# A graph layer with gathered tiles: the first two units swapped, and the first residual loads issued at the end of the first stage

## The chip, the cores and the metric

One core of one Trainium2 chip. The metric is the time of one execution in microseconds (us) on the device; each number is a median with its range over several executions. Ratios are computed as the mean time of one kernel's fast runs over the mean of the other's fast runs of the same rounds, with a 95% interval, so they are not quite the ratio of the medians quoted.

## The reference, cut to what matters

```python
B, N, F_IN, F_OUT = (8, 4096, 256, 256)
HW = jnp.einsum('bnf,fo->bno', H, W)
A_norm = jax.nn.relu((A + A.T) * 0.5)
D = jnp.sum(A_norm, axis=1)
D_safe = jnp.where(D > 0, D, 1.0)
d_inv_sqrt = jnp.where(D > 0, D_safe ** (-0.5), 0.0)
DAD = d_inv_sqrt[:, None] * A_norm * d_inv_sqrt[None, :]
L_norm = jnp.eye(N, dtype=H.dtype) - DAD
out = jnp.einsum('nm,bmo->bno', L_norm, HW)
return jax.nn.relu(out)
...
x = _layernorm(x + _L0_gnn_ref(x, L0_gnn_W, adj), axis=-1)
```

The adjacency A is sparse. The 4096 nodes are 32 blocks of 128 rows.

## The kernel before: the parts that matter

In the first stage the adjacency is symmetrised on VectorE and written to HBM, superblock by superblock (four blocks each). The degrees follow from row sums. x times W is scaled by `r`, the inverse root of the degree, and written to HBM as `g_dram`. The last ten blocks are formed before their degree is known: they are *held*, and `release` scales and writes them once it is. Block 0's output is summed along the way in a PSUM tile, `lead`.

```python
for i in range(NS):
    for j in range(i, NS):
        ...                               # load, symmetrise, sum rows
    degrees(i)                            # deg, none, e, r, minus_r, minus_e
    for m in range(i * A, (i + 1) * A):
        if m in held:
            release(m)                    # scale by r, write to g_dram, queue its matmuls into lead
    ...
    elif i < 6:
        pieces = spread_early(i - 4)      # index lists of unit 0, then of unit 1
        for n in range(5):
            due.append([1 + n // 2, next, (pieces, None)])
        due.append([1 if i == 5 else 4, collect_index, (i - 4,)])
```

In the second stage the other 31 blocks are done in 16 *units* of two (the last of one). Each unit has some 20 tiles. A tile is two gathers started by GpSimd: 128 rows of the adjacency (`ga`) and 128 rows of `g_dram` (`g`, 1 MB) into one of 13 ring buffers. TensorE multiplies them into `py`. A block is then evicted by ScalarE, added to its residual rows `xr` (1 MB of x), normalised and written.

```python
def residual(i, ypool):
    xr = ypool.tile([P, B, F], F32, tag="xr", name=f"xr_{i}", bufs=4)
    nc.scalar.dma_start(xr, x[:, i * P : (i + 1) * P, :].rearrange("b p f -> p b f"))
    return xr
...
ring = [gath.tile([P, G], F32, tag=f"g{k}", name=f"g{k}", bufs=1) for k in range(RING)]   # RING = 13
steps = [(u, step) for u in range(NU) for step in steps_of(u)]
...
for n in range(RING):
    gather(n)
xr = {}
...
after(3, residuals, [0])                  # xr of block 0, issued by ScalarE
finish(0)                                 # evict lead
for q, (u, step) in enumerate(steps):
    if new:
        after(10 if u + 1 < NU else 4, residuals, range(2 * u + 1, 2 * u + 1 + blocks(u)))
```

## Time and profile before

| | before |
|---|---|
| median of 3 runs | 1635.83 us (1634.33 to 1635.96) |
| end of the first stage (last matmul of `lead`) | 586 us |
| sixth gathered tile landed | 613.8 us |
| TensorE without a gap | 613.9 to 1001 us |

The lines these come from are shown and read in the prediction below. A windows line reads: stretch, length, then busy time of each engine with its number of instructions, then granted TensorE clock (1.00 is full), DMA share and GB/s.

### The profile page before, as it was taken

The page shows a single profiled execution, that of the slowest core. Times are in us where ns is not written, and L with a number is a line of the kernel's source. Part 1 is how long each engine was busy: PE and PEld are TensorE (multiplying, and loading weights), DVE is VectorE, ACT ScalarE, POOL GpSimd, SP SyncE. Part 2 cuts the span into 40 slices and gives each one's busy share as a digit, 9 for nine tenths or more (in the row PEclk, how much of TensorE's full clock was granted, in tenths as well). Part 3 has the DMA queues.
Part 4 walks back from the last instruction along what each step waited for, and adds up shares of the span by engine and source line. Part 5 has one row for each costly group of instructions (what it writes and reads, how often), then busy time and mean ns, then how long its engine had stood idle before and what let it go on. Part 6 is the DMA issues. An engine that isn't in the chain of part 4 may idle for free.

```text
span 1631.2 us, 18596 instructions
## 1 busy us (share of the span) xinstructions
PE 1491.2 (91%) x6544; PEld 787.1 (48%) x6544; DVE 810.5 (50%) x1886; ACT 365.0 (22%) x454; POOL 792.8 (49%) x1116
## 2 busy tenths in 40 slices
PE   6999989898899969999999999897979989999893
PEld 5787877776677624334343333333323333343331
DVE  5666578665465530052616527525635624545244
ACT  3555545444444410010100100100001001010110
POOL 3010010101011156477777767767767767777662
PEclk9999999999989989999999999999999999999997
DMA  9999999998788699889999999999999899999995
GB/s 352 374 370 389 392 375 376 400 368 333 290 320 329 258 360 405 298 291 397 327 404 377 370 370 379 365 367 349 345 361 337 323 382 335 378 387 369 357 355 188
DMA packets 229715, 575.13 MB, mean 353 GB/s; under 512 B 20473, under 2 KB 119081, under 8 KB 191945
## 3 DMA queue, kind: packets, MB, share of 16 engines
q0 software_dynamic: 56672, 305.12, 48.9%
q1 hardware_dynamic: 100912, 134.23, 23.4%
q10 hardware_dynamic: 72032, 134.51, 22.0%
q8 instruction: 55, 0.90, 0.2%
q14 instruction: 44, 0.36, 0.1%
HBM read 479.07 MB, written 136.34 MB: 377 GB/s over the span
## 4 chain that ended last, share of the span: by engine, by line
PE 57%; DMA 23%; issue 7%; DVE 6%; POOL 5%; ACT 1%; POOLq 0%; SPq 0%; DVEq 0%; ACTq 0%
PE py L805 34%; DMA g<-g_dram,gi 18%; PE pg L437 10%; PE lead L400 5%; PE tr L342 3%; PE xtr L426 3%; DVE sym L345 2%; DMA a_dram<-sym 2%; POOL g L663 2%; POOL ga L652 2%; DMA xin<-in_x_dram 1%; DMA adj<-in_adj_dram 1%; DVE part L350 1%; ACT sym L349 1%; POOL rstd L589 1%
## 5 line engine op out<-in xcount | busy, mean ns | idle before, releaser
L805 PE MATMUL py<-g,ga 128*64 128x512 f32 (+1 forms) x3152 | 938.3, 607 | 71.7 <-DMA g<-g_dram,gi 60.6
L805 PEld LDWEIGHTS py<-g,ga 128*64 128x64 f32 (+1 forms) x3152 | 350.8, 156 | 646.5 <-issue 630.5
L663 POOL DMA_INDIRECT g<-g_dram,gi x302 | 341.9, 1132 | 199.6 <-DMA g<-g_dram,gi 67.4
L652 POOL DMA_INDIRECT ga<-a_dram,ai x302 | 327.9, 1086 | 96.1 <-issue 83.4
L565 ACT ACTIVATE y<-py,minus_r 128x512 f32<-128x512 f32 x120 | 78.5, 687 | 922.5 <-PE py L805 646.9
L591 DVE TENSOR_SCALAR xr<-xr,mv,rstd 128x256 f32<-128x256 f32 x256 | 89.4, 419 | 299.1 <-POOL rstd L589 299.1
L437 PE MATMUL pg<-w_sb,xt 128*128 128x256 f32 x1024 | 231.8, 385 | 0.9 <-DVE sym L345 0.9
L437 PEld LDWEIGHTS pg<-w_sb,xt 128*128 128x128 f32 x1024 | 196.0, 194 | 29.3 <-issue 2.4
L345 DVE TENSOR_TENSOR sym<-tr,adj 128x512 f32<-128x512 f32 x256 | 163.7, 684 | 81.3 <-PE tr L342 77.9
L350 DVE TENSOR_REDUCE part<-sym 128x32 f32<-128x2048 f32 x64 | 145.5, 2281 | 61.1 <-ACT sym L349 61.0
L395 POOL DMA_DIRECT2D strip<-a_dram x32 | 18.3, 573 | 316.4 <-PE lead L400 309.8
L342 PE MATMUL tr<-ident,adj 128*128 128x128 f32 x1024 | 135.9, 283 | 21.3 <-DMA adj<-in_adj_dram 10.7
L349 ACT ACTIVATE sym<-sym 128x2048 f32<-128x2048 f32 x64 | 122.5, 1915 | 117.6 <-DVE sym L345 111.8
L342 PEld LDWEIGHTS tr<-ident,adj 128*128 128x128 f32 x1024 | 118.4, 145 | 49.6 <-DVE sym L345 22.5
L576 DVE TENSOR_TENSOR xr<-xr,y 128x2048 f32<-128x2048 f32 (+1 forms) x35 | 73.7, 2106 | 69.5 <-ACT y L565 64.6
L167 DVE TENSOR_TENSOR_SCAN incl_r<-carry,lists 128x32 f32<-128x32 f32 x13 | 2.8, 219 | 196.0 <-PE lists L236 196.0
L426 PE MATMUL xtr<-ident,xin 128*128 128x128 f32 x512 | 74.6, 292 | 21.9 <-DVE sym L345 18.2
L581 DVE BATCH_NORM_STATS2 stats<-xr 128x6 f32<-128x256 f32 x256 | 87.2, 411 | 0.8
L370 POOL TENSOR_TENSOR r<-e,neg_half 128x4 f32<-128x4 f32 x8 | 8.3, 1041 | 161.7 <-DVE e L369 155.6
L267 DVE TENSOR_TENSOR hot<-iota_q,at 128x1024 bf16<-128x1024 f32 x64 | 76.4, 1219 | 14.1 <-PE lead L400 12.9
L400 PE MATMUL lead<-gt,strip 128*128 128x512 f32 x176 | 83.3, 593 | 0.0
L427 ACT COPY xt<-xtr 128x512 f32<-128x512 f32 x128 | 69.3, 589 | 49.9 <-PE xtr L426 48.8
(104 smaller groups left out, 639.8 us busy)
## 6 DMA issues: line engine op xcount, KB each, us to landing
adj<-in_adj_dram SPq DMA_DIRECT2D x64, 1024.0 KB, 10.6
a_dram<-sym ACTq DMA_DIRECT2D x64, 1024.0 KB, 9.4
xin<-in_x_dram SPq DMA_DIRECT2D x64, 512.0 KB, 11.6
xr<-in_x_dram ACTq DMA_DIRECT2D x32, 1024.0 KB, 25.0
out_dram<-xr SPq DMA_DIRECT2D x31, 1024.0 KB, 24.4
g_dram<-gt ACTq DMA_DIRECT2D x22, 1024.0 KB, 7.0
g_dram<-held ACTq DMA_DIRECT2D x10, 1024.0 KB, 9.7
ga<-a_dram,ai POOLq DMA_INDIRECT x302, 9.6
```

What stands on the lines that cost most here:

```text
L342: nc.tensor.transpose(pt[:, c * P : (c + 1) * P], tji[:, c, a * P : (a + 1) * P], ident)
L345: nc.vector.tensor_add(sym[:, a, :], pt, tij[:, a, :])
L349: nc.scalar.activation(sym, sym, AF.Relu, scale=0.5)
L350: nc.vector.tensor_reduce(part[:, i * A : (i + 1) * A, j * S // Q : (j + 1) * S // Q], sym.rearrange("p a (c q) -> p a c q", q=Q), AX.X, A ...
L400: nc.tensor.matmul(lead[c], lhsT=strip, rhs=g[:, c * S : (c + 1) * S], start=not done, stop=len(done) == NB - 1, skip_group_check=True,)
L426: nc.tensor.transpose(pt[:, k, c, :], xin[b // H][:, b % H + k, c * P : (c + 1) * P], ident)
L437: nc.tensor.matmul(pg[:, k * FO : (k + 1) * FO], lhsT=xt[:, b + k, c, :], rhs=w_sb[:, c, :], start=(c == 0), stop=(c == FC - 1),)
L581: nc.vector.bn_stats(stats[:, b, :], z[:, b, :])
L591: ins = nc.vector.tensor_scalar(z[:, b, :], z[:, b, :], mv[:, b, 0:1], rstd[:, b : b + 1], ALU.subtract, ALU.mult,)
L652: tail["pool"] = nc.gpsimd.indirect_dma_start(out=at if both else at[:, :P], out_offset=None, in_=a_pairs if both else a_rows, in_offset=b ...
L663: tail["pool"] = nc.gpsimd.indirect_dma_start(out=gt, out_offset=None, in_=g_dram, in_offset=bass.IndirectOffsetOnAxis(ap=gi[:, t : t + 1] ...
L805: tail["pe"] = nc.tensor.matmul(py[2 * u + 1 + b][c][rows, :], lhsT=at[:, off + rows.start : off + rows.stop], rhs=gt[:, c * S : (c + 1) * S],
```

## The change

It is meant to fill idle DMA time at the boundary of the stages and to keep the boundary's gathers free of other loads. The residual rows of block 0 and of the first unit are now loaded by SyncE's queue, before the first gathers. And the units go in the order 1, 0, 2, 3 and on, unit 1 having 24 tiles and unit 0 having 29. The diff, cut to its core (`prepare` and `lists` only get the new order's names):

```diff
+SEQ = [1, 0, *range(2, 16)]
...
-                for u in range(3):
-                    due.append([1 + u, count_place_rest, (u,)])
+                for n, u in enumerate(SEQ[:3]):
+                    due.append([1 + n, count_place_rest, (u,)])
             elif i < 6:
-                pieces = spread_early(i - 4)
+                pieces = spread_early(SEQ[i - 4])
...
-                due.append([1 if i == 5 else 4, collect_index, (i - 4,)])
+                due.append([1 if i == 5 else 4, collect_index, (SEQ[i - 4],)])
...
-    def residual(i, ypool):
+    def residual(i, ypool, engine=None):
...
-        steps = [(u, step) for u in range(NU) for step in steps_of(u)]
+        steps = [(u, step) for u in SEQ for step in steps_of(u)]
...
+        xr = {
+            i: residual(i, ypool, nc.sync) for i in (0, *range(2 * SEQ[0] + 1, 2 * SEQ[0] + 1 + blocks(SEQ[0])))
+        }
         for n in range(RING):
             gather(n)
-        xr = {}
...
-        after(3, residuals, [0])
         finish(0)
...
-                after(10 if u + 1 < NU else 4, residuals, range(2 * u + 1, 2 * u + 1 + blocks(u)))
+                if q > 0:
+                    after(10 if u != SEQ[-1] else 4, residuals, range(2 * u + 1, 2 * u + 1 + blocks(u)))
```

More of the change, by code (lines that the diff above doesn't have):

```diff
@@ L554 @@
                 pass
-    def residual(i, ypool):
+    def residual(i, ypool, engine=None):
         xr = ypool.tile([P, B, F], F32, tag="xr", name=f"xr_{i}", bufs=4)
-        nc.scalar.dma_start(xr, x[:, i * P : (i + 1) * P, :].rearrange("b p f -> p b f"))
+        (engine or nc.scalar).dma_start(xr, x[:, i * P : (i + 1) * P, :].rearrange("b p f -> p b f"))
         return xr
@@ L731, in residuals @@
                     xr[i] = residual(i, ypool)
+        ahead = {u: {k: SEQ[n + k] for k in (2, 3, 4) if n + k < NU} for n, u in enumerate(SEQ)}
         def prepare(u):
-            if u + 2 < NU:
+            if 2 in ahead[u]:
+                v = ahead[u][2]
                 for _ in spread(
-                    u + 2,
-                    lpool.tile([P, NB, P], BF16, tag="hot", name=f"hot_{u + 2}", bufs=1),
-                    lpool.tile([P, NB, tmax], F32, tag="inn", name=f"inn_{u + 2}", bufs=1),
-                    lpool.tile([P, NB, 2, tmax], BF16, tag="val", name=f"val_{u + 2}", bufs=1),
-                ):
-                    pass
-            if u + 4 < NU:
-                patterns(u + 4)
+                    v,
+                    lpool.tile([P, NB, P], BF16, tag="hot", name=f"hot_{v}", bufs=1),
+                    lpool.tile([P, NB, tmax], F32, tag="inn", name=f"inn_{v}", bufs=1),
+                    lpool.tile([P, NB, 2, tmax], BF16, tag="val", name=f"val_{v}", bufs=1),
+                ):
+                    pass
+            if 4 in ahead[u]:
+                patterns(ahead[u][4])
         def lists(u):
@@ L751, in lists @@
             pr = one[:, w : w + 2 * NB].rearrange("p (k m) -> p k m", k=2)
-            if u + 4 < NU:
-                count(u + 4, tot, low)
-            if u + 3 < NU:
-                count_rest(u + 3, pr[:, 0], pr[:, 1])
-            if u + 2 < NU:
-                pl = two[:, w : w + 2 * tiles[u + 2]].rearrange("p (k t) -> p k t", k=2)
-                collect(u + 2, pl)
-                index(u + 2, pl)
-            if u + 3 < NU:
-                place_rest(u + 3, pr[:, 0], pr[:, 1])
-            if u + 4 < NU:
-                place(u + 4, tot, low)
-        after(3, residuals, [0])
+            if 4 in ahead[u]:
+                count(ahead[u][4], tot, low)
+            if 3 in ahead[u]:
+                count_rest(ahead[u][3], pr[:, 0], pr[:, 1])
+            if 2 in ahead[u]:
+                v = ahead[u][2]
+                pl = two[:, w : w + 2 * tiles[v]].rearrange("p (k t) -> p k t", k=2)
+                collect(v, pl)
+                index(v, pl)
+            if 3 in ahead[u]:
+                place_rest(ahead[u][3], pr[:, 0], pr[:, 1])
+            if 4 in ahead[u]:
+                place(ahead[u][4], tot, low)
         finish(0)
```

## The prediction

> **What bounds the kernel now.** I read the page first, then a table by stage, then the chain of waits around the change of stage, then the waits of TensorE and GpSimd in the second stage. The page says that this is a kernel in which two things are nearly full at once:
>
> ```profile
> PE   6999989898899969999999999897979989999893
> PEclk9999999999989989999999999999999999999997
> DMA  9999999998788699889999999999999899999995
> ```
>
> The first stage (adjacency symmetrised, x multiplied by W, block 0 summed) ends at about 586 us; the second (302 gathered tiles of 1 MB, in 16 units) fills the rest. Both PE and DMA read 9 nearly everywhere in the second stage, so I split it, with PE busy, its clock, the DMA share and GB/s as the columns to watch:
>
> ```profile
> 555.00:558.00 3.00, 0.97 (x32) 0.85 (x31) 3.00 (x5) 1.97 (x1) 1.00 (x1) 1.00 0.32 125
> 558.00:570.00 12.00, 11.91 (x28) 5.44 (x29) 9.60 (x22) 4.45 (x4) 4.25 (x9) 1.00 1.02 405
> 570.00:582.00 12.00, 12.00 (x29) 5.33 (x28) 3.10 (x6) 3.50 (x2) 2.20 (x4) 1.00 1.01 403
> 582.00:585.00 3.00, 3.00 (x8) 1.33 (x7) 0.00 (x0) 1.37 (x2) 0.00 (x0) 1.00 0.80 320
> 585.00:588.00 3.00, 0.82 (x2) 0.00 (x0) 2.03 (x2) 1.37 (x2) 2.31 (x2) 1.00 0.20 28
> 588.00:600.00 12.00, 1.96 (x4) 0.34 (x4) 10.44 (x24) 0.00 (x0) 9.87 (x8) 0.62 1.03 372
> 600.00:614.00 14.00, 10.27 (x34) 3.25 (x36) 0.00 (x0) 0.00 (x0) 10.32 (x11) 0.84 1.03 403
> 614.00:665.00 51.00, 51.00 (x123) 21.82 (x124) 2.87 (x8) 0.00 (x0) 35.91 (x36) 0.97 1.00 389
> 665.00:705.00 40.00, 40.00 (x138) 14.64 (x137) 3.06 (x4) 2.75 (x4) 17.88 (x17) 1.00 0.73 267
> 705.00:782.00 77.00, 77.00 (x292) 30.03 (x291) 27.84 (x89) 4.81 (x7) 53.57 (x47) 1.00 0.95 364
> 782.00:1000.00 218.00, 218.00 (x922) 83.06 (x922) 110.99 (x334) 19.44 (x29) 166.45 (x145) 1.00 0.99 371
> 1000.00:1600.00 600.00, 546.09 (x2126) 209.45 (x2123) 271.63 (x826) 51.46 (x80) 425.22 (x372) 0.97 0.96 359
> ```
>
> Three regimes are to be seen. From 586 to 614 TensorE starves while DMA is full. From 614 to 1000 PE is busy in every microsecond, so PE sets the pace. From 1000 on PE has gaps (546 of 600 us) and DMA is at 0.96: DMA sets it. The chain of waits shows where the first regime ends, and the PE stretches of units 0 and 1 after it:
>
> ```profile
> 603.44 10.33 DMA g<-g_dram,gi
> 613.77 0.14 issue
> 613.90 90.87 PE py L805 x254
> ...
> 705.93 76.03 PE py L805 x256
> ```
>
> The gather issued at 603.44 is the sixth; the first five were issued from 586.73 on. Once it has landed, at 613.77, PE never waits again until 1001. So the landing of the sixth gather is the number that a change at the boundary must move. GpSimd's waits between 655 and 710 us tell what the DMA's dip there is:
>
> ```profile
> POOL g L663 <- PE py L805: 21.4, 8, 4.6
> ```
>
> GpSimd waits for PE to free one of the 13 ring buffers: the ring is full, and DMA is idle because PE is slower there, not for want of anything to fetch.
>
> [...] the three residual loads, issued on ScalarE's queue from 585.87 to 588.85 us, landed 6.4, 14.4 and 32.2 us after issue, beside gathers whose own latency was 8.3 to 11.3 us (median 10.0) until 615, against a median of 5.8 between 675 and 706 where DMA has room. [...] GpSimd's gather instructions take about 1.0 us elsewhere but 1.4 to 2.9 us while VectorE works between 586 and 595.
>
> **The change part by part.**
>
> *Residuals moved.* Three loads of 1 MB (blocks 0, 1, 2, from 585.87) leave the boundary. Three others (0, 3, 4; blocks 3 and 4 are the first unit's now) go to SyncE's queue, idle after its last input load at 524.37, and start when their buffers come free. These take over memory of the first stage, in its adjacency buffers. The last users there are the index matmuls that end at 556.7 and the last symmetrising adds on VectorE, which end at 563.2. So I expect one load at about 551 to 557 and the rest from 563.
>
> What do they meet there? Ten held tiles of 1 MB are written to HBM; eight of them are issued between 558.07 and 575 and the last lands at 585.46, on which the first gather waits (GpSimd waits 7.9 us for it, to 585.38). The table shows DMA share 1.02 and 1.01 from 558 to 582. So 3.1 MB at 405 GB/s, 7.8 us of all engines, goes into a stretch that is full, and not into the hole of 540 to 558, unless a buffer is freed early.
>
> *What that is worth.* Count DMA work up to the landing of the sixth gather. It is nearly the same set of bytes before and after; what can be won is idle time. From 557 on that is: one microsecond at share 0.32, 0.7 us; 582 to 585 at 0.80, 0.6 us; 585 to 588 at 0.20, 2.4 us. Sum 3.7 us. The hole at 585 to 588 is the restart between the last write and the first gather's packets; it does not vanish, because the first gather still waits for the writes, but it moves and may be partly filled by late residual packets; I give back 1.5 us for it. The third old load landed only at 619, after the sixth gather, so a part of it, some 0.25 MB or 0.6 us, was not in the old count and is in the new. Sum: 3.7 - 1.5 - 0.6 = 1.6 us earlier.
>
> *Check by the issue side.* With the loads in the way, the last held write lands some 5 to 6 us later, at 591, and the first gather's issue goes from 586.73 to about 592.5. The sixth comes five pairs later: 5 x 2.56 us (0.94 + 0.30 + 1.00 + 0.30, plus rounding, from the undisturbed pairs) = 12.8 us, plus about 1.5 us for VectorE's remaining interference: 606.8. With the unloaded latency of 5.8 us it lands at 612.6, or 1.2 us earlier. Both ways say 1 to 2 us.
>
> *Order 1, 0.* Both units begin with the same seven half tiles, so the starving start is alike. PE time of the two together is a sum, 90.87 + 76.03 and the same first steps, whatever the order. What the order moves is when the ring fills. Before, unit 0 (29 tiles, seven of the dearest kind) came first and filled the ring by 665; DMA then lost (1 - 0.73) x 40 = 11 us. After, unit 1 (24 tiles) needs about 24 x 2.8 = 67 us of DMA plus one 1 MB output in 76 us of PE; it stays fed but gains only some 6 tiles of lead; unit 0 then brings the ring to its cap of 13. Either way the ring is about full when both are done, so the lost 11 us are not recovered: the later starvation is put off only by lead carried over, and that is capped. I book 0, with 1 tile, 2.8 us, either way.
>
> *The rest.* Index lists keep their places by position in the order; the removed issue slots on ScalarE (0.4 us each) were not on the chain. 0.
>
> Sum: -1.6 us at the boundary. It should carry through to the end, since both regimes after it start earlier by the same amount with the same ring. From 1635.8 this gives 1634. Because the residual buffer freed first might catch the hole before 558 (1 MB there is worth 2.6 us), I lean a little lower: 1633.
>
> **The rivals.** First, full relief: the loads land without delaying the writes. Then gathers start at 586.73 with no residuals beside them; GpSimd issues the sixth at 603.44 as before, and it lands 5.8 us later, at 609.2: 4.6 us won, 1631. For it speaks the share of about 0.3 to 0.6 before 558; against it the buffers' release at 563. Second, the loads turn into a longer wait for the held writes: 7.8 us later gathers with a second clock ramp of PE (granted clock 0.62 between 588 and 600) gives a loss of 3 to 5 us, 1640. For it speaks the saturated stretch; against it the same 3.1 MB missing later. Third, the order keeps DMA busy where it idled and the whole 11 us come back at the end: 1623. Against it speaks the cap of 13 buffers.
>
> **Range and chances.** The terms are a few microseconds each, against a spread of 1.6 us in the three runs. I take 1633, with 1626 to 1639 for 8 times in 10. Two per cent is 33 us; no term above, nor all together in either direction, comes to that: faster 0.02, same 0.96, slower 0.02.
>
> **What would show it right or wrong.** Right: residuals issued by SyncE between 550 and 575; the last held write and with it the first gather some 5 us later than 586.7; the first gathers with a latency of 6 to 8 us in place of 10; PE unbroken from about 612 on; the full-ring dip at 665 to 705 gone or moved to about 740 to 780. Wrong: first gather at 586.7 (then the first rival); PE gaps inside unit 1 (the ring runs dry, slower); DMA share clearly higher from 614 to 800 and the first starvation much later than 1001 (the third rival).

## More of the kernel before

Different sessions fell on different chips; their numbers (3, 8, 9, 12, 15) are used as names only.

The source line numbers move between kernels, because lines were added; names are what to go by.

## The result, and the profile after

The changed kernel took 1652.62 us (median of 4 runs, 1651.29 to 1654.05); the kernel before 1635.89 (4 runs, 1634.33 to 1640.65, three of them from earlier, one from that session). The ratio is 1.0097, interval 1.0074 to 1.0121. This is within 2%, but 13.6 us above the top of the predicted range, and the sign is the other one.

The profile of that run, busy tenths in 40 slices of the span, to set beside the lines of the same names at the head of the prediction:

```profile
PE   6999989898899868999999999989988989999894
PEclk9999999999899987999999999999999999999997
```

The sixteenth slice (620 to 661 us) has PE at 8 with a granted clock of 7; before, both were 9. One window of the same kernel (columns as before) says how much:

```profile
614.00:665.00 51.00, 42.89 (x90) 16.46 (x87) 2.86 (x8) 0.00 (x0) 33.72 (x34) 0.83 0.99 385
```

Before, TensorE was busy for all 51 us with 123 matmul passes; here it did 90 passes, and unit 2 starts at 811.2 us instead of 797.0. The profiled executions have spans of 1652.3 and 1631.2 us, so 14.2 of 21.1 us are lost by then and 7 later. The timeline of PE in that window (start, length, what, and in brackets the idle time before it and what ended it) shows how:

```profile
621.11 14.21 PE L815 MATMUL py<-g,ga 128*128 128x512 f32 x32 [0.16 <-DMA g<-g_dram,gi]
636.83 0.59 PE L815 MATMUL py<-g,ga 128*128 128x512 f32 x1 [1.51 <-issue]
638.93 1.01 PE L815 MATMUL py<-g,ga 128*128 128x512 f32 x1 [1.51 <-issue]
...
651.58 36.26 PE L815 MATMUL py<-g,ga 128*128 128x512 f32 x111 [1.11 <-issue]
```

Passes that are normally 0.43 us apart start 0.8 to 2.8 us apart. Most of their distances are multiples of 0.70 us (636.83, 638.93: 3 x 0.70). "issue" means that the profile shows nothing that the engine waited for; a wait whose release was not recorded would read the same, and records are missing in this trace, as is told below. But all the passes of one tile need the same two gathers, and these gaps lie inside a tile, so it is no late tile. The clock of 0.83 comes from 17.1 us at half clock (granted 0.50) that begin at 638.7, four us after the slow stretch began. TensorE had been busy for 1.18 of the 4.0 us before (634.7 to 638.7), so I take the half clock for a consequence; that is my reading, and no run isolates it. A good part of the loss comes through it: the gaps themselves sum to 7.5 us. TensorE, not DMA, is what was late: DMA was at 0.99.

Nothing in the diff acts on a running matmul. So the first question was whether this belongs to the kernel at all, and the second what the change does where it does not happen.

### The profile page after: what moved, and what is told of

Same layout as the page of the kernel before. It is cut to its first block, busy times and chain, and to the rows that moved or that the text cites. A ratio compares the mean times of both kernels' runs of the same rounds, so it can differ in the third digit from the quotient of the medians.

```text
span 1652.3 us, 18595 instructions
## 1 busy us (share of the span) xinstructions
PE 1504.6 (91%) x6544; PEld 791.3 (48%) x6544; DVE 812.1 (49%) x1886; ACT 364.6 (22%) x454; POOL 783.8 (47%) x1116
## 4 chain that ended last, share of the span: by engine, by line
PE 58%; DMA 22%; issue 7%; DVE 6%; POOL 5%; ACT 2%; POOLq 0%; SPq 0%; DVEq 0%; another core or an unknown queue 0%; ACTq 0%
PE py L815 37%; DMA g<-g_dram,gi 15%; PE pg L439 9%; PE lead L402 5%; DMA a_dram<-sym 4%; PE tr L344 3%; PE xtr L428 3%; DVE sym L347 2%; POOL ga L654 2%; DMA xin<-in_x_dram 2%; POOL g L665 2%; DMA adj<-in_adj_dram 1%; DVE part L352 1%; ACT sym L351 1%; POOL rstd L591 1%
## 5 line engine op out<-in xcount | busy, mean ns | idle before, releaser
L815 PE MATMUL py<-g,ga 128*64 128x512 f32 (+1 forms) x3152 | 950.7, 607 | 74.9 <-DMA g<-g_dram,gi 48.0
L815 PEld LDWEIGHTS py<-g,ga 128*64 128x64 f32 (+1 forms) x3152 | 355.5, 155 | 657.4 <-issue 639.2
L665 POOL DMA_INDIRECT g<-g_dram,gi x302 | 336.8, 1115 | 214.1 <-PE py L815 78.1
L654 POOL DMA_INDIRECT ga<-a_dram,ai x302 | 323.1, 1070 | 96.5 <-issue 83.7
L344 PE MATMUL tr<-ident,adj 128*128 128x128 f32 x1024 | 136.3, 283 | 20.9 <-DMA adj<-in_adj_dram 10.2
L428 PEld LDWEIGHTS xtr<-ident,xin 128*128 128x128 f32 x512 | 60.7, 149 | 41.6 <-DVE sym L347 29.2
```

Source lines behind the costliest of these rows:

```text
L344: nc.tensor.transpose(pt[:, c * P : (c + 1) * P], tji[:, c, a * P : (a + 1) * P], ident)
L428: nc.tensor.transpose(pt[:, k, c, :], xin[b // H][:, b % H + k, c * P : (c + 1) * P], ident)
L654: tail["pool"] = nc.gpsimd.indirect_dma_start(out=at if both else at[:, :P], out_offset=None, in_=a_pairs if both else a_rows, in_offset=b ...
L665: tail["pool"] = nc.gpsimd.indirect_dma_start(out=gt, out_offset=None, in_=g_dram, in_offset=bass.IndirectOffsetOnAxis(ap=gi[:, t : t + 1] ...
L815: tail["pe"] = nc.tensor.matmul(py[2 * u + 1 + b][c][rows, :], lhsT=at[:, off + rows.start : off + rows.stop], rhs=gt[:, c * S : (c + 1) * S],
```

## The experiments

Stage 1 varies by several us from run to run before the change can act. I therefore count landmarks from the first write of a held tile, which fell at 512 to 521 us in all profiles. The table is for looking up; `lead` is the block of 64 matmuls that multiplies the held tiles, and "unit 2" is the start of the third unit in time, when the same work is done in every variant.

| kernel, chip | `lead` starts | PE idle before it | `lead` lasts | unit 2 | landing records | median us (kernel before there) |
|---|---|---|---|---|---|---|
| before, first profile | +41.8 | 1.36 | 27.7 | +280.7 | 15387 | 1635.83 |
| before (e5), 3 | +41.9 | 1.36 | 27.7 | +281.1 | 15380 | 1633.79 (1634.84) |
| before (e11), 12 | +42.8 | 1.36 | 27.7 | +281.1 | 15379 | 1632.07 (1633.52) |
| changed, first measurement | +45.3 | 4.35 | 29.4 | +296.3 | 12066 | 1652.62 (1635.89) |
| changed (e1), 9 | +46.5 | 4.35 | 29.9 | +282.0 | 15373 | 1634.96 (1634.20) |
| changed (e6), 3 | +44.8 | 4.35 | 30.6 | +280.9 | 15382 | 1635.27 (1634.84) |
| changed (e12), 12 | +46.2 | 4.35 | 30.0 | +281.6 | 15370 | 1634.53 (1633.52) |
| changed (e10), 8 | +45.8 | 4.35 | 29.2 | +294.3 | 11938 | 1654.41 (1637.23) |
| changed (e16), 15 | +48.7 | 4.35 | 30.5 | +297.9 | 12539 | 1652.95 (1639.89) |
| order only (e2), 9 | +46.4 | 4.35 | 29.9 | +287.3 | 15382 | 1641.17 (1634.20) |
| loads only (e3), 9 | +42.3 | 1.36 | 27.7 | +278.3 | 15387 | 1631.48 (1634.20) |
| lists kept (e14), 12 | +42.2 | 1.36 | 27.7 | +278.3 | 15388 | 1631.77 (1633.52) |
| lists kept (e7), 8 | +42.2 | 1.36 | 27.7 | +285.0 | 11817 | 1646.49 (1637.23) |
| lists kept, loads late (e8), 8 | +42.3 | 1.36 | 27.7 | +280.3 | 11814 | 1645.97 (1637.23) |
| lists swapped only (e9), 8 | +45.4 | 4.35 | 29.3 | +285.7 | 11889 | 1645.00 (1637.23) |

"Landing records" is the number of semaphore records of DMA landings that I counted in the trace; 15392 are due.

### Does it happen again, and what part does what (e1 to e4, one chip)

Theory X: the slow stretch is an accident of that measurement. Theory P: it is the program's. The changed kernel unaltered:

> The changed kernel once more, unaltered. In its first profile the whole loss at the start of the third unit (14.2 us) sat in two steps of the first unit, where TensorE's passes, 0.43 us each elsewhere, came 0.7 to 2.8 us apart from 634 to 652 us with no wait named. Theory P (the program's order or placement makes those two steps slow): the slow stretch is there again, in the same two steps, 13 to 16 us long, and the time is 1650 to 1655. Theory X (an accident of that one profile, the loss is elsewhere in the other runs): the two steps take 6.9 us each and the time is still some 16 us over before.

Measured: 1634.96 us (1634.28 to 1636.8, 4 runs), ratio 1.002 (0.9978 to 1.0061), no slow stretch, all landing records there. Theory P falls, at least on this chip.

The order alone:

```diff
-        xr = {i: residual(i, ypool, nc.sync) for i in (0, 3, 4)}   # written out
+        xr = {}
...
+        after(3, residuals, [0])
         finish(0)
...
-                if q > 0:
+                if True:
```

> Units in the order 1, 0, with the residual loads left on ScalarE's queue where the kernel before has them. If the order makes the loss: 1649 to 1655, with the slow stretch in the first unit. If the moved loads make it: within 4 us of before (1632 to 1640) and no slow stretch. My prediction booked 0 for the order.

Measured: 1641.17 us (1636.76 to 1643.62), ratio 1.0046 (1.0001 to 1.0091), unit 2 at +287.3 against +281 before. The order, with the lists that are swapped along with it, costs 6 us, where I had booked 0. The large loss that this run and the next two were to divide did not occur on this chip.

The loads alone:

```diff
-SEQ = [1, 0, *range(2, 16)]
+SEQ = [*range(16)]
```

> Units in the order 0, 1, with the residual loads of blocks 0, 1 and 2 on SyncE's queue at the end of the first stage. If the moved loads make the loss: 1648 to 1655, with a slow stretch of TensorE some 20 to 50 us after the second stage starts. If the order makes it: 1631 to 1638, as my prediction had it for the loads (1.6 us earlier).

Measured: 1631.48 us (1628.3 to 1634.12), ratio 0.9988 (0.9945 to 1.0031); unit 2 at +278.3. The loads win 2.8 us by the landmark; in the time that is too small for the interval.

The changed kernel with the early loads issued by ScalarE:

```diff
-            i: residual(i, ypool, nc.sync) for i in ...
+            i: residual(i, ypool, nc.scalar) for i in ...
```

> The changed kernel with the early residual loads issued by ScalarE in place of SyncE. If SyncE's queue (a third stream of packets, or its place in the order of issue) matters: the loss shrinks to under 8 us. If the order or the early bytes alone matter: 1649 to 1655 as the changed kernel.

Measured: 1634.78 us (1632.9 to 1641.31), ratio 1.0025 (0.9978 to 1.0073); unit 2 at +283.9, 1.9 to 3 us behind the changed kernel. The third load was issued at 586.1 instead of 582.4 us (e1). In the time it is not told apart. What SyncE's queue has to do with the large loss stays open.

### How large is the noise (e5, e6, another chip)

> The kernel before against itself: what the timing resolves. Both theories expect a ratio within 0.3% of 1 and no slow stretch of TensorE; its profile also gives the first stage and the sixth gather's landing of the kernel before on this chip, to set beside the changed kernel's. If the start of the held writes (558.07 us in the first profile of before, 559.5 to 564.0 in five profiles of changed programs) is drift, it lies near 562 here; if the change delays the first stage, it stays near 558.

Measured: the kernel before against itself 1.0000 (0.997 to 1.0029), single runs from 1628.58 to 1642.89 us. A few us in single runs mean nothing here. The first held write after the pause (558.07 us in the first profile) was issued at 559.03 and not near 562, so it is the change that delays it.

> The changed kernel a third time. Theory X (the 1652.6 us of the first measurement belongs to that measurement, in which TensorE stood 0.7 to 2.8 us between passes with no wait and a fifth of the records of landings was lost): 1632 to 1638, a ratio of 0.997 to 1.005, no slow stretch, landings' records complete. Theory P (the program is prone to it): at least one of the six runs at 1648 or more.

Measured: 1635.27 us (1629.9 to 1638.53, 6 runs), ratio 1.0001 (0.9973 to 1.003), no slow stretch. Where it does not happen, the two kernels are equal. Windows of this profile, against the same lines of before in the prediction:

```profile
614.00:665.00 51.00, 49.42 (x132) 20.30 (x132) 2.86 (x8) 0.00 (x0) 36.55 (x38) 1.00 1.00 403
665.00:705.00 40.00, 40.00 (x199) 14.12 (x196) 24.74 (x68) 5.50 (x8) 30.82 (x24) 1.00 0.96 358
...
745.00:782.00 37.00, 37.00 (x127) 13.60 (x126) 0.00 (x0) 1.85 (x3) 15.79 (x16) 1.00 0.66 235
```

The dip of the full ring has moved from 665 to 705 (share 0.73) to 745 to 782 (0.66), as predicted, and nothing is won by it, as predicted.

### Why the order costs (chain and timelines of e5 and e6)

The chain of waits of the changed kernel in e6 (start, length, what):

```profile
562.20 30.62 PE lead L402 x64
...
592.84 0.70 ACT y L567
...
593.58 0.26 POOL g L665
...
608.40 7.45 DMA g<-g_dram,gi
...
615.99 58.94 PE py L815 x174
```

The sixth gather's latency fell from 10.3 to 7.45 us, as the change means it to. But it was issued later: 91.0 us after the first held write, against 87.7 in e5, because the first gather waits for the eviction of `lead`, and `lead` ends later. `lead` starts later and lasts 30.6 us instead of 27.7. PE just before it, first in e5 (before), then in e6 (changed), same chip:

```profile
556.73 0.97 PE L288 MATMUL pl<-mixed,hot 128*128 128x48 bf16 x32 [1.59 <-DVE sym L345]
559.06 8.42 PE L400 MATMUL lead<-held,strip 128*128 128x512 f32 x19 [1.36 <-ACT held L461]
```

```profile
556.78 1.07 PE L290 MATMUL pl<-mixed,hot 128*128 128x58 bf16 x32 [1.70 <-DVE sym L347]
562.20 5.49 PE L402 MATMUL lead<-held,strip 128*128 128x512 f32 x6 [4.35 <-ACT held L463]
```

PE waits 4.35 us for the scaled held tile instead of 1.36. The granted clock goes with it: where TensorE idled for 4.35 us, it fell to 0.50 for 6.8 us (10.2 in e4 and e13), which made the block 1.5 to 3 us longer; where it idled for 1.36 us there was no such stretch. The moment of the fall differed: in e6 it came at 561.2 us, 3.3 us after the idling began, in e1 1.9 us after it (562.3) and in e4 at once (559.0). What sets that moment these runs do not show. Why the tile is late is in VectorE's timeline, again e5 and then e6:

```profile
554.96 0.61 DVE L283 TENSOR_SCALAR mixed<-mixed,iota_p 128x768 bf16<-128x768 f32 x1
...
555.68 0.16 DVE L369 TENSOR_TENSOR e<-deg,none 128x4 f32<-128x4 f32 x1
...
555.99 0.69 DVE L345 TENSOR_TENSOR sym<-tr,adj 128x512 f32<-128x512 f32 x1
556.60 2.27 DVE L350 TENSOR_REDUCE part<-sym 128x32 f32<-128x2048 f32 x1
```

```profile
555.36 0.69 DVE L285 TENSOR_SCALAR mixed<-mixed,iota_p 128x928 bf16<-128x928 f32 x1
...
556.04 0.68 DVE L347 TENSOR_TENSOR sym<-tr,adj 128x512 f32<-128x512 f32 x1
556.64 2.27 DVE L352 TENSOR_REDUCE part<-sym 128x32 f32<-128x2048 f32 x1
558.84 0.15 DVE L371 TENSOR_TENSOR e<-deg,none 128x4 f32<-128x4 f32 x1
```

The list piece `mixed` is 928 wide instead of 768, since the lists that are spread second are now those of unit 0, with 29 tiles instead of 24. In the built program, the degree step `e` then stands behind a symmetrising add and a reduction of 2.27 us, where it stood ahead of them. `e` comes at 558.84 instead of 555.68; GpSimd's `r`, the scaling of the held tile and `lead` follow. The longer list pieces are not the cost (0.69 us against 0.61 in the lines shown); the changed place of a tiny instruction in VectorE's program is. It gives a test: keep the lists in the old order and change only the units.

### The lists apart from the order (e7, e8, e9; then e14)

Theory L: the swapped lists delay `lead`. Rival M: the order of the units itself costs. The edit for the changed kernel with lists kept:

```diff
+LISTS = [0, 1, 2]
...
-                for n, u in enumerate(SEQ[:3]):
+                for n, u in enumerate(LISTS):
...
-                pieces = spread_early(SEQ[i - 4])
+                pieces = spread_early(LISTS[i - 4])
...
-                due.append([1 if i == 5 else 4, collect_index, (SEQ[i - 4],)])
+                due.append([1 if i == 5 else 4, collect_index, (LISTS[i - 4],)])
```

> The changed kernel, but with the index lists of the first units prepared in the old order (unit 0's, then unit 1's), so that the degree step of the seventh superblock keeps its place on VectorE; the units' order and the early residual loads stay as changed. Theory L (the order costs time because the swapped lists delay that degree step, hence the block of 64 matmuls): the block starts about 42 us after the first write of the held tiles, with TensorE idle 1.4 us before it and no stretch at half clock near 560, it lasts about 27.7 us, unit 2 starts at +278 to +280, time 1629 to 1633. Rival M (the units' order itself costs, by unit 1 first being ahead of its tiles): block at +45 to +46.5, unit 2 at +281 to +282, time 1635, as in the changed kernel.

The same with the loads late, as in e2:

> Units in the order 1, 0, residual loads as in the kernel before (ScalarE's queue, later), lists prepared in the old order. Theory L: nothing is left that differs on the path, so as the kernel before: block at +42, idle before it 1.4 us, unit 2 at +280 to +282, time within 3 us of the kernel before. Rival M: unit 2 at about +287, 4 to 6 us slower, as the run with the order alone.

Only the lists swapped (`SEQ = [*range(16)]`, `LISTS = [1, 0, 2]`, loads late):

> Units in the old order 0, 1, residual loads as in the kernel before, only the preparation of the first units' lists swapped (unit 1's first). Theory L: this alone makes the delay: block at +45 to +46.5 with TensorE idle over 4 us before it, a stretch of 6 to 7 us at half clock near 560, the block 30 us long, unit 2 at +285 to +287, 4 to 6 us slower than the kernel before. Rival M: as the kernel before, unit 2 at +281.

The session fell on chip 8, where times turned out disturbed (1646.49, 1645.97 and 1645.00 us; ratios 1.004, 1.0034 and 1.0045), so only the landmarks decide. They do so as theory L has it in all three. With lists kept, `lead` is at +42.2 and +42.3 after 1.36 us of idling; with lists swapped and nothing else changed, it is at +45.4 after 4.35 us, with a half clock for 6.8 us from 557.0. Unit 2 of e8 is at +280.3, as in the kernel before: up to there the order of the units by itself costs nothing. Unit 2 of e9 is at +285.7, 4.6 us late. The times I had expected were missed: all three are slower than the kernel before on this chip, e8 by 8.7 us in the median. Its profiled run lost its time after unit 2, and no run of e8 on a quiet chip tells what of this is the chip's.

On a quiet chip, e7 again:

> The changed kernel with the lists in the old order, again. On a chip without the stall: block of 64 matmuls at +42, no half clock, sixth-tile step at +100, unit 2 at +278 to +279, time 2 to 4 us below the changed kernel's and 1 to 4 below the kernel before. On a losing chip: those landmarks up to the sixth-tile step, then some microseconds lost without a named wait.

Measured on chip 12: `lead` at +42.2, unit 2 at +278.3 as expected, no half clock near 560; PE before `lead`:

```profile
558.61 8.85 PE L403 MATMUL lead<-held,strip 128*128 128x512 f32 x20 [1.36 <-ACT held L464]
```

The time was 1631.77 us (1628.49 to 1639.84), the kernel before 1633.52, ratio 0.9991 (0.9962 to 1.0021). The median lies 1.8 us below the kernel before's and 2.8 below the changed kernel's; by the interval it is the same. It is the best form of the change that I found, with the loads alone (e3) its equal: unit 2 at +278.3 in both, with the new order and with the old. In its trace `e` is ahead of the add again (555.24 and 555.54 us).

### What holds TensorE (e10 to e13, e15 to e17)

The same session on chip 8 ran the unaltered changed kernel:

> The changed kernel unaltered, a fourth time, on whichever chip this is. If the stretch in which TensorE began one instruction per 0.70 us belongs to the kernel: 1650 to 1655 with that stretch at about 634 to 652. If it belonged to the session of the first measurement: 1632 to 1638, no gap over 0.3 us in TensorE's work without a named wait, some 15380 records of landings.

Measured: 1654.41 us (1651.65 to 1666.39, 4 runs), ratio 1.012 (1.0077 to 1.0162), unit 2 at +294.3. The stretch is back, on the same grid:

```profile
627.71 3.17 PE L815 MATMUL py<-g,ga 128*128 128x512 f32 x7
631.67 0.59 PE L815 MATMUL py<-g,ga 128*128 128x512 f32 x1 [0.80 <-issue]
633.76 0.59 PE L815 MATMUL py<-g,ga 128*128 128x512 f32 x1 [1.50 <-issue]
```

So theory X in its first form falls too: it was no accident of one measurement. It comes with the chip, or with the session: only chip 9 was used in two sessions, so the two are not told apart. And the measurements on chip 8 show a second sign. The page's list of DMA issues gives a time to landing only where the landings are in the trace; e6 and then e10:

```profile
a_dram<-sym ACTq DMA_DIRECT2D x64, 1024.0 KB, 9.4
```

```profile
a_dram<-sym ACTq DMA_DIRECT2D x64, 1024.0 KB
```

In the first measurement, on chip 8 and on chip 15, 11,800 to 12,500 of the 15,392 landing records are there; on chips 3, 9 and 12 at least 15,370. No loss is to be seen before the first gather at about 590 us. The loss is greatest about where TensorE is held, or just before: from 620 to 640 us e10 has 36 landing records, e6 has 224; e8, which is not held there, has 80. The records of instructions are complete in both (18595).

Next, the profile of the kernel before, and the changed kernel once more:

> The kernel before against itself, to have its profile on this chip. If the chip is one that loses records of landings (about 11900 of 15390): TensorE gaps without a named wait in it too, from 920 us on, and none at 600 to 660, where it waits for tiles anyway. If not: none, and all records there. Ratio 1.000 within 0.4% either way.

> The changed kernel unaltered. On a chip with all landing records: 1633 to 1638, no gaps without a wait, unit 2 at +281 after the first held write. On a chip that loses them: 1650 to 1656 with a slow stretch between 630 and 655, unit 2 at +294.

These runs fell on chip 12. Both traces are complete and neither shows a slow stretch: 1632.07 us (ratio 0.9981, 0.995 to 1.0011) for the kernel before against itself, 1634.53 (1.0002, 0.9966 to 1.0037) for the changed one.

To see whether more instructions bring the stretch or lengthen it (theory R), or whether their number makes no difference (rival F), I added 240 tiny copies on ScalarE:

```diff
         finish(0)
+        for _ in range(240):
+            nc.scalar.copy(dose, ident[:, :1])
```

> The changed kernel plus 240 copies of one column on ScalarE right after the eviction of block 0, where ScalarE is idle until about 669: some 40 us of work that nothing waits for. Theory R [...]: on a losing chip the stretch gets longer, by 5 us or more over the fifth run of the changed kernel; on a chip that loses none it may appear. Rival F [...]: as the changed kernel in the same session, within 3 us.

This run missed its aim. In the built program 223 of the copies lay in ScalarE's idle time of stage 1, for nothing tied them to the boundary, and the chip was a quiet one: 1627.09 us (1626.35 to 1638.2), ratio 0.9977 (0.9938 to 1.0015). Its first held write came at 512.1 us, earlier than in any other run; I do not know why, and the interval does not part it from 1. It says nothing on the question. The dose again, with copies that cannot start before block 3's residual rows have landed:

```diff
         finish(0)
+        for _ in range(280):
+            nc.scalar.copy(dose, xr[3][:, 0, :1])
```

> The changed kernel plus 280 copies of one column of block 3's residual rows on ScalarE, at some 599 to 647 us. Theory R [...]: on a chip that loses records the slow stretch is longer by 5 us or more than in the changed kernel of the same call; on one that loses none it may appear, or records begin to be missing in 600 to 650. Rival F [...]: as the changed kernel within 3 us, no stretch on a chip that loses none.

> The changed kernel unaltered: 1629 to 1639 with all records of landings, or 1650 to 1656 with the slow stretch on a chip that loses them.

These runs fell on chip 15, which loses records too. The changed kernel took 1652.95 us (2 runs; ratio 1.0078, 0.999 to 1.0166), the one with the dose 1653.38 (2 runs; ratio 1.0081, 1.0051 to 1.011). Unit 2 came at +297.9 and +296.3. The stretch did not get longer by 5 us, so theory R's number was missed; the times, 0.4 us apart, are what rival F had given. But ScalarE was held as well, and that is more telling than the length. Its timeline first, then parts of all engines' together (PEld is TensorE's weight load):

```profile
603.36 23.20 ACT L778 COPY dose<-xr 128x1 f32<-128x1 f32 x104
```

```profile
643.01 1.00 POOL L666 DMA_INDIRECT g<-g_dram,gi  x1 [0.61 <-issue]
643.22 0.59 PE L818 MATMUL py<-g,ga 128*128 128x512 f32 x1 [0.87 <-issue]
643.23 0.19 ACT L778 COPY dose<-xr 128x1 f32<-128x1 f32 x1 [1.21 <-ACT dose L778]
...
644.62 0.19 PEld L818 LDWEIGHTS py<-g,ga 128*128 128x128 f32 x1 [2.60 <-issue]
644.63 0.19 ACT L778 COPY dose<-xr 128x1 f32<-128x1 f32 x1 [1.21 <-ACT dose L778]
645.32 0.59 PE L818 MATMUL py<-g,ga 128*128 128x512 f32 x1 [1.52 <-issue]
645.34 0.19 ACT L778 COPY dose<-xr 128x1 f32<-128x1 f32 x1 [0.51 <-ACT dose L778]
645.87 1.00 POOL L666 DMA_INDIRECT g<-g_dram,gi  x1 [0.61 <-issue]
```

Until 627 us ScalarE does a copy of 0.19 us every 0.22 us, 104 in a row. Then it goes onto the grid of 0.70 us, alone at first, while TensorE's passes still come every 0.43 us. From 642 us on both are held, copies and matmuls and weight loads starting at the same instants, until they are let go together at 656 us. GpSimd is not slowed: its gathers of `g` come 2.86 us apart there, as in e6. The copies read one column of SBUF; once block 3's rows have landed they need no DMA, no PSUM and nothing of TensorE's. Nor is it the clock that holds ScalarE: the granted clock was 1.00 from 627 to 643 us, where ScalarE was on the grid already. What the two engines have in common is the grid of 0.70 us; what it comes from, no trace names.

The runs do not settle it. The dose did not lengthen the hold, and e8 loses as many landing records as e10 (11814 and 11938 are there) and is not held at 620 to 660 us. A late supply of instructions would be one candidate, but the traces show no sign of it: between 500 and 800 us the fetches in the instruction queue q8 (which names no engine) are eight in the profile of before and eight in that of the first measurement, 16 KB each, 0.92 to 1.13 us long in the one and 0.88 to 1.19 us in the other; and from 600 to 660 us q8 moved one packet in e6 and one in e10. I leave the cause open.

The last run was to show whether the kernel before is held there too:

> The kernel before, one look. On a chip that loses records of landings: gaps in TensorE's work without a named wait from about 920 us on, as in the other kernels there; at 630 to 660 few or none, since its second unit is short of tiles until about 660. On a chip that loses none: no such gap anywhere.

It fell on chip 9, which keeps its records: 1634.97 us (one run), 15382 landing records, no gap without a named wait. So the profile of the kernel before on a losing chip is missing. What can be said of such chips: without the early loads (e8 and e9) there is no held stretch between 600 and 660 us, though there are short ones from 920 us on, 17 us of gaps in all in e8 and 13 in e9; with the early loads it is there in the four runs with swapped lists (6 to 10 us of gaps) and, in e7, with 4 us of gaps. Why it takes the early loads to bring it on, I cannot show: e8 runs TensorE without a gap and DMA at 411 to 412 GB/s from 620 to 660 us as well, and is not held.

## Why the prediction was wrong

It must be judged twice: on the chips that keep their landing records, and on those that lose them.

**Where nothing holds the engines (chips 3, 9, 12) the time was right, by luck in part: two errors in the sum offset each other.** The 14 runs of the changed kernel there lie between 1629.41 and 1639.32 us, 13 of them in the range; the medians are 1634.5 to 1635.3, predicted 1633, and each is equal to the kernel before in its session.

- "Once it has landed, at 613.77, PE never waits again": right; in e6 the sixth tile lands at 615.85 and PE runs on from 615.99. But the two stretches of 90.87 and 76.03 us are not units 0 and 1: they end at list matmuls some steps into the next unit, and unit 1 ended at 797.0 us.
- The loads "start when their buffers come free", "one load at about 551 to 557 and the rest from 563": wrong. They were issued from 578.4 to 580.3 us (e6) and landed by 599.2. The chain of e14 shows them waiting for a write of the symmetrised adjacency to land (lines below this list). So they do not delay the held writes by "some 5 to 6 us": with the lists kept or the order unchanged, the last held write lands at +71.5 instead of +69.2 to +70.9.
- The worth of the loads, "1.6 us earlier": TensorE's work on the sixth tile begins 0.8 to 2.5 us earlier (+96.8 in e3 and e14, +97.6 to +99.3 in four profiles of before), which is the size predicted, though not by the road predicted; at unit 2 it is 2.8 us (+278.3, against +281.1). The first gathers' latency, predicted 6 to 8 us, was 7.45 (e6), 6.3 (e3) and 8.6 (e14) for the sixth.
- "Order 1, 0 ... I book 0": right of the order itself (e8, +280.3; e14 no later than e3).
- "Index lists keep their places by position in the order ... 0": the step that failed. They keep their places, but they are lists of other sizes, and with them the built order of VectorE's program changed: `e` about 3 us later, PE idle 4.35 us, half a clock for 6.8 us. The first gather, which the prediction has waiting for the held writes, then waits for the eviction of `lead` (in e6, where the last held write lands at 589.7, until 593.54 us). Alone this costs 4.6 us (e9), and 3.2 us on top of the loads (+281.5, the mean of e1, e6 and e12, against +278.3). I took a count of instructions for their cost and did not ask what stands behind them.
- The dip that moves and wins nothing: right, to 745 to 782 us.

```profile
565.71 9.85 DMA a_dram<-sym
...
575.70 13.05 DMA xr<-in_x_dram
```

So the sum on these chips is not -1.6 but -2.8 + 3.2 = +0.4 us.

**On the chips that lose records (8, 15, and that of the first measurement, by its 12,066 landing records) it was wrong: the medians, 1652.6 to 1654.4, lie 20 to 21 us above 1633.** The step that failed is "It should carry through to the end, since both regimes after it start earlier by the same amount with the same ring". The mechanism it lacked: unit 2 came at +294.3 to +297.9 instead of +281, since TensorE was held for 13 to 18 us in the middle of its first unit (631 to 656 us), and more was lost after unit 2 (7 us in the first measurement). What holds it stays open; in the runs here it was held only in such sessions, and between 600 and 660 us only with the early loads. Nothing in the profile of before, taken on a chip that keeps its records, could show that. But the range was drawn from "a spread of 1.6 us in the three runs", and that was too bold: the kernel before alone goes from 1625.68 to 1649.13 us over the chips, and its medians by session from 1633.5 to 1639.9 (one single run besides, 1632.63).

## What to carry to other kernels

Before a cost of 0 is booked for work that only changes places, look which tiny instruction on the path stands behind it on the same engine: here a step of 0.16 us, moved behind 2.9 us of other work, cost 3 to 5 us, part of it through the clock. When a result will not fit any wait in the profile, repeat it in another session, on another chip, before explaining it, and compare landmarks inside the trace rather than whole times. And look whether the trace itself is complete: missing landing records (at most 12,539 of 15,392 there, against at least 15,370) were the sign by which the disturbed sessions could be told.
